# Output projection as seven products of half blocks, with layer 0's division on ScalarE and its rows read back from DRAM

## The chip, the cores and the metric

The kernel runs on one core of a Trainium2 chip. The metric is the device time of a whole execution in microseconds (us). TensorE (PE in the profile; PEld is its weight load) multiplies matrices into PSUM, VectorE (DVE) and ScalarE (ACT) do elementwise work, GpSimd (POOL) does small work here, and SyncE (SP) issues the DMAs.

## The reference

Two layers of attention over 64 graphs of 256 nodes with 512 features, all float32, eight heads of 64. Each layer adds its input and normalises:

```python
# layer 0: graph attention
feats = einsum('bnf,hfu->bhnu', X, W)
dense = leaky_relu(e_self[..., :, None] + e_neigh[..., None, :], 0.2) - 1e10 * (1 - A)
out0 = relu(einsum('bhij,bhju->bhiu', softmax(dense), feats) + b)
x = layernorm(x + out0)
# layer 1: attention mixed with adjacency and distance (both are adj here)
q, k, v = split(x @ W_qkv)
attn = softmax(q @ k.T * 64**-0.5) * 0.33 + 0.33 * adj + 0.33 * exp(-adj)
x = layernorm(x + (attn @ v) @ W_out + b_out)
```

(The node mask, all ones in the inputs, also enters layer 1.)

## The kernel before

The loop at the end of the kernel runs over the graphs b = 1 to 63 and calls two functions per round, between a `start` for the first two graphs and an `end`. One round works on four graphs at once: layer 0's attention of b, layer 0's projections of b + 1, layer 1's projections and scores of b - 1, and layer 1's values, output projection and normalisation of b - 2 and b - 3. Each call `do(stage, b, step)` emits one step of one stage, and `in_order` (L86) then ties each engine's instructions to the order of the source. So every engine's order is the order in which the `do` lines stand, and a step placed earlier or later moves on all engines that it uses.

The projections of both layers are done by `seven` (L289): a product of two matrices cut into half blocks, done in seven products of half blocks and additions, instead of eight products. `left_factors` (L273) forms four sums of the activation's half blocks on VectorE (`xC`, `hC`), and `right_factors` (L215) the same for weights, once. In `seven`, the products p1, p6, p7 and p4 add up one after the other in one PSUM bank ("chain"); ScalarE copies the bank (L309) after each of them, so that each copy must be done before the next of these products may write. p2 has a bank of its own, p5 and p3 share a third, and `add` (L312) adds these onto the copies on VectorE:

```python
BANK = dict(p1="chain", p6="chain", p7="chain", p4="chain", p2="alone", p5="pair", p3="pair")
COPIES = dict(p1=11, p6=12, p7=22, p4=21)
ADDED = {11: "alone", 22: "pair", 12: "pair"}
```

The output projection `project` (L1004) is a plain one: for each of the two blocks of 128 rows, four products of 128 x 128 with 128 x 512 into one bank. (A float32 product is two instructions in the profile.) `sum_up` (L932) adds the residual, which lies in `X1[b]`, straight from PSUM.

The other steps that this text names: `scores` (L811) computes the scores of two heads and ScalarE exponentiates them (L826); `pairs` (L834) adds two blocks of them; `values` (L916) multiplies weights and values, ScalarE copies the result to `oT` (L930). `rows` (L477) turns two columns of layer 0's features into rows and takes their maximum on VectorE; `broadcast` (L488) exponentiates them on ScalarE ("grow", L490) and sends them through DRAM to all partitions. `row_sums` (L857) and `invert` (L863) compute the inverse row sums of layer 1's softmax and send them through DRAM ("rb"). `columns` (L540) forms layer 0's column factors ("nd", then "ccol" on ScalarE), `scaled` (L607) scales the features on ScalarE, `weights` of layer 0 (L641) forms the attention weights `pT` on VectorE (L650), and `product` (L661) multiplies. `norm0` (L681) divides by the row sums: a reciprocal (L686) and a multiplication (L688), both on VectorE, into `X1[b]`. `end` (L694) adds the input, and `squares` and `norm` normalise on ScalarE with small steps on POOL. `weights` of layer 1 (L903) multiplies the probabilities by the inverse row sums and adds the common part. `rows_to_blocks` (L773) stores layer 0's rows to a DRAM buffer `hs` and reads them back in blocks `hb`, which VectorE transposes to `hT` (L121).

SBUF and PSUM buffers come from pools: a tile with a tag and `bufs=n` waits until one of its n buffers is released. [...] At the end of a round, `ps_tile([P, F], f"turn_{b}")` takes an "mm" buffer without using it.

## Time and profile before

| | us |
|---|---|
| median of 3 runs | 2964.55 (2962.11 to 2969.35) |
| profiled execution | 2961.33 |
| its span, first to last instruction | 2959.6 |
| TensorE busy | 2922.9 |
| VectorE busy | 2609.2 |
| ScalarE busy | 1468.1 |
| GpSimd busy | 185.6 |

The mean granted TensorE clock is 0.994. The DMA queues moved 328 MB. Busy times of different engines overlap; only the engine that is never idle, or a chain of waits between engines, sets the end. A line number such as L300 in a profile line is one of the kernel before; the changed kernel's numbers are some 8 to 90 higher.

### The profile page before, as it was taken

Reading aid. Unit: us, or ns where it says so; the run is one execution under the profiler, and the core shown is the slowest. Engines: PE = TensorE matmul, PEld = TensorE weight load, DVE = VectorE, ACT = ScalarE, POOL = GpSimd, SP = SyncE. Lnnn points to the kernel's source line nnn. Section 1 sums busy time; section 2 is a strip of 40 time slices with the busy share of each in tenths; the row PEclk is TensorE's granted clock in tenths of the full one; section 3 lists DMA queues with packets and bytes.
Section 4 is the critical chain, followed back from the end, with each engine's and each line's share of the span. In section 5 each row is a group of like instructions: output and inputs, shape, how many; then the busy total and the mean of one; then the engine's idle time right before and its main releaser. Section 6 shows DMA issues by size and latency. Waiting matters only on the chain.

```text
span 2959.6 us, 64542 instructions
## 1 busy us (share of the span) xinstructions
PE 2922.9 (99%) x25526; PEld 2321.6 (78%) x25526; DVE 2609.2 (88%) x5151; ACT 1468.1 (50%) x3585; POOL 185.6 (6%) x526
## 2 busy tenths in 40 slices
PE   8999999999999999999999999999999999999998
PEld 6787877877878878778778778778788787787785
DVE  5898898898998988989988988989889889889884
ACT  2445555555455455455555554554554554555443
POOL 0000000000000000000000000000000000000000
PEclk8999999999999999999999999999999999999999
DMA  6344454454444444444544543544444445445421
GB/s 137 79 121 109 106 130 104 103 137 95 112 128 102 114 116 105 124 109 106 130 107 105 132 101 106 134 98 112 122 104 118 111 107 126 109 105 131 102 87 50
DMA packets 760611, 328.20 MB, mean 111 GB/s; under 512 B 693516, under 2 KB 694268, under 8 KB 744312
## 3 DMA queue, kind: packets, MB, share of 16 engines
q1 hardware_dynamic: 758200, 323.55, 44.0%
q8 instruction: 204, 3.34, 0.5%
q14 instruction: 95, 0.78, 0.1%
q10 hardware_dynamic: 2112, 0.52, 0.1%
HBM read 256.13 MB, written 67.61 MB: 109 GB/s over the span
## 4 chain that ended last, share of the span: by engine, by line
PE 96%; DVE 1%; DMA 1%; issue 0%; ACT 0%; SPq 0%; POOL 0%; POOLq 0%; DVEq 0%
PE pq_p L300 27%; PE po L1007 15%; PE pv_p L300 13%; PE pf_p L300 13%; PE av L673 8%; PE pz L817 8%; PE av L922 8%; PE pd L846 2%; PE pr L82 1%; PE pg L531 0%; SPq L114 0%; DMA gb<-gs 0%; DMA rb<-rs 0%; DMA x<-in_x_dram 0%; DMA xb<-in_x_dram 0%
## 5 line engine op out<-in xcount | busy, mean ns | idle before, releaser
L300 PE MATMUL pq_p<-hC,wqk_sb 128*128 128x128 f32 x4096 | 489.1, 278 | 6.0 <-ACT qk L309 3.9
L300 PEld LDWEIGHTS pq_p<-hC,wqk_sb 128*128 128x128 f32 x4096 | 470.6, 193 | 11.8 <-ACT qk L309 4.7
L1007 PE MATMUL po<-wo_sb,oT 128*128 128x512 f32 x1024 | 450.0, 592 | 0.0
L650 DVE SCALAR_TENSOR_TENSOR pT<-gb,ccol,at 128x256 f32<-128x256 f32 x992 | 403.2, 478 | 17.5 <-ACT ccol L549 17.5
L351 ACT ACTIVATE junk<-x,nmean_l 128x512 bf16<-128x512 f32 x256 | 185.0, 722 | 418.5 <-POOL nmean_l L346 414.4
L300 PEld LDWEIGHTS pq_p<-hT,wqk_sb 128*128 128x128 f32 x3072 | 355.0, 193 | 28.7 <-issue 25.5
L300 PE MATMUL pq_p<-hT,wqk_sb 128*128 128x128 f32 x3072 | 372.7, 278 | 2.1 <-DVE hT L121 0.7
L826 ACT ACTIVATE p<-pz,hide 128x512 f32<-128x512 f32 x512 | 309.8, 688 | 123.8 <-PE av L922 106.1
L1007 PEld LDWEIGHTS po<-wo_sb,oT 128*128 128x128 f32 x1024 | 189.7, 190 | 216.5 <-issue 200.2
L912 DVE TENSOR_TENSOR p<-p,ct 128x1024 f32<-128x1024 f32 x252 | 308.7, 1225 | 8.6
L309 ACT COPY qk<-pq_p 128x512 f32<-128x512 f32 x256 | 147.2, 575 | 328.2 <-PE pq_p L300 328.2
L905 DVE TENSOR_TENSOR p<-p,rb 128x1024 f32<-128x1024 f32 x252 | 304.2, 1207 | 5.3 <-DMA rb<-rs 5.3
L309 ACT COPY v<-pv_p 128x256 f32<-128x256 f32 x256 | 95.3, 372 | 336.2 <-PE pv_p L300 336.2
L673 PE MATMUL av<-v,pT 128*64 128x65 f32 x8192 | 256.6, 223 | 3.7 <-issue 2.9
L817 PE MATMUL pz<-qk 64*128 64x256 f32 x2048 | 256.3, 389 | 2.2 <-ACT p L826 2.1
L673 PEld LDWEIGHTS av<-v,pT 128*64 128x64 f32 x8192 | 246.8, 139 | 13.0 <-issue 5.3
L609 ACT ACTIVATE v<-v 128x64 f32<-128x64 f32 x1024 | 251.6, 337 | 0.0
L300 PE MATMUL pf_p<-wf_sb,xC 128*128 128x264 f32 x992 | 251.1, 386 | 0.0
L300 PE MATMUL pv_p<-wv_sb,hC 128*128 128x256 f32 x1024 | 242.3, 379 | 0.0
L817 PEld LDWEIGHTS pz<-qk 64*128 64x128 f32 x2048 | 187.1, 186 | 66.7 <-ACT p L826 27.3
L922 PE MATMUL av<-p,v 128*64 128x256 f32 x2016 | 231.7, 382 | 0.0
L300 PEld LDWEIGHTS pv_p<-wv_sb,hC 128*128 128x128 f32 x1024 | 194.4, 190 | 27.9 <-ACT v L309 0.4
(137 smaller groups left out, 3775.0 us busy)
## 6 DMA issues: line engine op xcount, KB each, us to landing
rb<-rs SPq DMA_DIRECT2D x63, 1024.0 KB, 5.4
gb<-gs SPq DMA_DIRECT2D x62, 1028.0 KB
xb<-in_x_dram SPq DMA_DIRECT2D x252, 128.0 KB, 5.6
x<-in_x_dram SPq DMA_DIRECT2D x63, 512.0 KB
hs<-x SPq DMA_DIRECT2D x63, 512.0 KB
hb<-hs SPq DMA_DIRECT2D x252, 128.0 KB, 3.4
out_dram<-x SPq DMA_DIRECT2D x63, 512.0 KB, 5.5
adj<-in_adj_dram SPq DMA_DIRECT2D x256, 64.0 KB, 4.4
```

What stands on the lines that cost most here:

```text
L300: matmul(d, lhsT, rhs, start=(p in FIRST and i == 0), stop=(i == len(todo) - 1), skip_group_check=True,)
L309: nc.scalar.copy(out[COPIES[p]], dst)
L351: nc.scalar.activation(junk, self.src[:, t, :], AF.Square, bias=self.nmean[:, t : t + 1], accum_out=self.rstd[:, t : t + 1],)
L609: nc.scalar.activation(V0[b][:, t, h, :U], V0[b][:, t, h, :U], AF.Copy, scale=V0[b][:, t, h, U : U + 1],)
L650: nc.vector.scalar_tensor_tensor(pT[h][:, j, :], GB[b][h], CCOL[b][:, j, h : h + 1], AT[b][:, j, :], op0=ALU.max, op1=ALU.mult,)
L673: matmul(av[r * half : (r + 1) * half, k, :], pT[h][:, j, i : i + half], V0[b][:, j, h, :UA], start=(j == 0), stop=(j == T - 1),)
L817: matmul(pz[:, r, j, :], QK[b][rows, g, 1, j * P : (j + 1) * P], QK[b][rows, g, 0, :], start=True, stop=True,)
L826: nc.scalar.activation(p[:, :, j, :], pz[:, :, j, :], AF.Exp, bias=hide[:, j, b : b + 1], scale=U**-0.5,)
L905: nc.vector.tensor_mul(p, p, REC[b][:, k : k + 2, g // 2, :] .unsqueeze(2) .to_broadcast([P, 2, T, N]),)
L912: nc.vector.tensor_add(p, p, CT[b].unsqueeze(1).to_broadcast([P, 2, T, N]))
L922: matmul(av[0][r * U : (r + 1) * U, g % 2, :], V1[b][:, j, 2 * g + r, :], PROBS[b][g][:, r, j, :], start=(j == 0), stop=(j == T - 1),)
L1007: matmul(po, oT[:, c, t * P : (t + 1) * P], wo_sb[:, c, :], start=(c == 0), stop=(c == C - 1),)
```

## The change

The output projection of graphs 0 to 61 goes through `seven_rows`: `half_blocks` forms the left factors of `oT` on VectorE, the products go to `o` (in the buffer of tag "xb", which the loads of the next input blocks use too), ScalarE copies and VectorE adds, and `sum_up` follows in the next round from SBUF. The last two graphs keep the plain form, with products 256 wide, since `wo_sb` now holds the seven right factors. Layer 0's rows, which were kept in `X1` with three buffers, are read back from `hs` into `Y[b]` for the residual, and `X1` has one buffer. The division of layer 0 is done on ScalarE from graph 2 on, as sixteen activations of 64 columns with the reciprocal as scale. The copy of the inverse row sums (`zd`) goes to ScalarE. In the order of the source, `bias`, `aT`, the left factors of x and of h, the loads of the next blocks and the store of layer 1 stand elsewhere, the squares of layer 0 are split in two, and the unused PSUM tile is gone.

```diff
@@ -158,3 +158,3 @@
     load_wf(nc.scalar, 0)
-    a_bc = io.tile([P, 2, H, U], FT, tag="x1", name="a_bc", bufs=3)
+    a_bc = io.tile([P, 2, H, U], FT, tag="x1", name="a_bc", bufs=1)
     for k, a in enumerate((a_self, a_neigh)):
@@ -181,3 +181,3 @@
     bo_bc = consts.tile([P, F], FT, name="bo_bc")
-    wo_sb = consts.tile([P, C, F], FT, name="wo_sb")
+    wo_sb = consts.tile([P, 7, C2, F2], FT, name="wo_sb")
 
@@ -232,2 +232,10 @@
 
+    def load_wo():
+
+        wo12 = work.tile([P, C2, F2], FT, tag="pT", name="wo12", bufs=4)
+        parts = w_out.rearrange("(k c p) (g f) -> k g p c f", k=2, p=P, g=2)
+        for dst, k, g in ((wo_sb[:, 0], 0, 0), (wo12, 0, 1), (wo_sb[:, 1], 1, 0), (wo_sb[:, 2], 1, 1)):
+            nc.sync.dma_start(dst, parts[k, g])
+        return wo12
+
     def load_weights1():
@@ -682,3 +690,3 @@
             if b not in X1:
-                X1[b] = io.tile([P, T, F], FT, tag="x1", name=f"x1_{b}", bufs=3)
+                X1[b] = io.tile([P, T, F], FT, tag="x1", name=f"x1_{b}", bufs=1)
             av = AV[g][:, t, : HG * UA].rearrange("p (h u) -> p h u", u=UA)
@@ -686,8 +694,18 @@
             nc.vector.reciprocal(rec, av[:, :, U])
-            s = slice(g * HG * U, (g + 1) * HG * U)
-            nc.vector.tensor_mul(
-                X1[b][:, t, s].rearrange("p (h u) -> p h u", u=U),
-                av[:, :, :U],
-                rec.unsqueeze(2).to_broadcast([P, HG, U]),
-            )
+            if b < 2:
+                s = slice(g * HG * U, (g + 1) * HG * U)
+                nc.vector.tensor_mul(
+                    X1[b][:, t, s].rearrange("p (h u) -> p h u", u=U),
+                    av[:, :, :U],
+                    rec.unsqueeze(2).to_broadcast([P, HG, U]),
+                )
+                return
+            for k in range(HG):
+                h = g * HG + k
+                nc.scalar.activation(
+                    X1[b][:, t, h * U : (h + 1) * U],
+                    av[:, k, :U],
+                    AF.Copy,
+                    scale=rec[:, k : k + 1],
+                )
 
...
@@ -730,3 +748,3 @@
             hb = io.tile([P, C, N // B, B], FT, tag="hb", name=f"hb_{b}", bufs=1)
-            hs = dram.tile([N, F], FT, tag="hs", name=f"hs_{b}")
+        HS[b] = dram.tile([N, F], FT, tag="hs", name=f"hs_{b}", bufs=4)
 
@@ -773,4 +791,5 @@
         def rows_to_blocks():
-            nc.sync.dma_start(hs.rearrange("(t p) f -> p t f", p=P), X1[b])
-            load_blocks(hb, hs)
+            nc.sync.dma_start(HS[b].rearrange("(t p) f -> p t f", p=P), X1[b])
+            if b > 0:
+                load_blocks(hb, HS[b])
 
@@ -778,3 +797,2 @@
             transpose_blocks(hT, hb)
-            left_factors(hC, hT)
 
@@ -876,3 +894,7 @@
             )
-            nc.vector.tensor_copy(zd, inv.unsqueeze(2).to_broadcast([P, K, B]))
+            nc.scalar.copy(zd, inv.unsqueeze(2).to_broadcast([P, K, B]))
+            PD["blocks"] = zd
+
+        def inverted():
+            zd = PD["blocks"]
             rec = work.tile([P, 2, N], FT, tag="rec1", name=f"rec1_{b}", bufs=1)
...
@@ -931,10 +955,16 @@
 
+        def rows_again():
+
+            tag = "y" if b < NB - 2 else "hb"
+            Y[b] = io.tile([P, T, F], FT, tag=tag, name=f"y_{b}", bufs=1)
+            nc.sync.dma_start(Y[b], HS[b].rearrange("(t p) f -> p t f", p=P))
+
         def sum_up(po, t):
             if t == 0:
-                NORM["l1", b] = LayerNorm(X1[b], b, "l1")
+                NORM["l1", b] = LayerNorm(Y[b], b, "l1")
             nc.vector.scalar_tensor_tensor(
-                X1[b][:, t, :],
+                Y[b][:, t, :],
                 po,
                 1.0,
-                X1[b][:, t, :],
+                Y[b][:, t, :],
                 op0=ALU.mult,
@@ -948,2 +978,21 @@
 
+        SEVEN = {}
+
+        def half_blocks():
+            oC = work.tile([P, 4, C2, P], FT, tag="xC", name=f"oC_{b}", bufs=1)
+            left_factors(oC, oT)
+            SEVEN["o"] = o = io.tile([P, T, F], FT, tag="xb", name=f"o_{b}", bufs=1)
+            SEVEN["product"], SEVEN["add"] = seven_rows(
+                f"po_{b}",
+                oT,
+                oC,
+                wo_sb,
+                [P, F2],
+                {
+                    10 * (t + 1) + g + 1: o[:, t, g * F2 : (g + 1) * F2]
+                    for t in range(T)
+                    for g in range(2)
+                },
+            )
+
         LAST = {}
@@ -999,4 +1048,6 @@
         def residual():
+            if b == NB - 1:
+                Y[b] = X1[b]
             nc.vector.tensor_add(
-                X1[b], X1[b], bo_bc.unsqueeze(1).to_broadcast([P, T, F])
+                Y[b], Y[b], bo_bc.unsqueeze(1).to_broadcast([P, T, F])
             )
@@ -1004,11 +1055,14 @@
         def project(t):
+
             po = ps_tile([P, F], f"po_{b}_{t}")
-            for c in range(C):
-                matmul(
-                    po,
-                    oT[:, c, t * P : (t + 1) * P],
-                    wo_sb[:, c, :],
-                    start=(c == 0),
-                    stop=(c == C - 1),
-                )
+            wo = [[wo_sb[:, 0], WO["12"]], [wo_sb[:, 1], wo_sb[:, 2]]]
+            for g in range(2):
+                for c in range(C):
+                    matmul(
+                        po[:, g * F2 : (g + 1) * F2],
+                        oT[:, c, t * P : (t + 1) * P],
+                        wo[c // C2][g][:, c % C2],
+                        start=(c == 0),
+                        stop=(c == C - 1),
+                    )
             sum_up(po, t)
...
@@ -1032,2 +1086,7 @@
             project=project,
+            rows_again=rows_again,
+            half_blocks=half_blocks,
+            product=lambda p: SEVEN["product"](p),
+            product_add=lambda i: SEVEN["add"](i),
+            sum_up=lambda t: sum_up(SEVEN["o"][:, t, :], t),
             squares=lambda *ts: NORM["l1", b].squares(*ts),
@@ -1117,2 +1176,3 @@
         do("proj1", 0, "from_rows", 1)
+        do("proj1", 0, "blocks")
         do("proj1", 0, "hC")
@@ -1145,3 +1205,3 @@
         if b > 1:
-            do("attend1", b - 3, "squares")
+            do("attend1", b - 4, "squares")
             do("proj1", b - 1, "qk", "p1")
@@ -1149,3 +1209,4 @@
             do("proj0", b, "columns")
-            do("attend1", b - 3, "store")
+            do("attend1", b - 4, "store")
+            do("attend1", b - 3, "rows_again")
             do("proj1", b - 1, "qk", "p6")
@@ -1162,2 +1223,4 @@
             do("proj1", b - 1, "qk_add", 22)
+            if b + 1 < NB:
+                do("turned", b + 1, "xC")
             do("attend1", b - 2, "weights", 0)
@@ -1170,15 +1233,16 @@
             nc.sync.dma_start(bo_bc, b_out.partition_broadcast(P))
-            nc.sync.dma_start(wo_sb, w_out.rearrange("(c p) f -> p c f", p=P))
+            WO["12"] = load_wo()
             in_order()
-        for g in range(2):
-            for t in range(T):
-                do("attend0", b, "norm0", g, t)
-        do("attend0", b, "end")
-        if b + 2 < NB:
-            load(b + 2)
+        for t in range(T):
+            do("attend0", b, "norm0", 0, t)
         if b > 1:
             do("proj1", b - 1, "qk", "p4")
+        for t in range(T):
+            do("attend0", b, "norm0", 1, t)
+        if b > 1:
             do("proj1", b - 1, "qk", "p3")
-            do("proj1", b - 1, "qk_add", 12)
         do("attend1", b - 2, "weights", 1)
+        if b > 1:
+            do("proj1", b - 1, "qk_add", 12)
+        do("attend0", b, "end")
         do("proj1", b - 1, "values", "p1")
@@ -1186,2 +1250,3 @@
         do("proj1", b - 1, "v_add", 11)
+        do("attend1", b - 3, "residual")
         do("proj1", b - 1, "values", "p6")
@@ -1190,9 +1255,15 @@
         do("proj1", b - 1, "v_add", 22)
+        for t in range(T):
+            do("attend1", b - 3, "sum_up", t)
+        if b + 2 < NB:
+            load(b + 2)
         do("proj0", b + 1, "product", "p1")
         do("proj1", b - 1, "values", "p4")
+        do("attend1", b - 2, "weights", 2)
+        do("attend0", b, "squares", slice(0, 1))
         do("proj0", b + 1, "product", "p6")
+        do("attend0", b, "squares", slice(1, 2))
         do("proj1", b - 1, "values", "p3")
-        do("attend0", b, "squares")
-        do("attend1", b - 2, "weights", 2)
         do("proj1", b - 1, "v_add", 12)
+        do("proj0", b + 1, "aT")
         do("proj0", b + 1, "product", "p5")
@@ -1205,4 +1276,2 @@
         do("proj0", b + 1, "product", "p2")
-        do("proj0", b + 1, "add", 11)
-        do("proj0", b + 1, "aT")
         if b + 2 < NB:
@@ -1213,2 +1282,3 @@
         do("attend1", b - 2, "weights", 3)
+        do("proj0", b + 1, "add", 11)
         do("proj0", b + 1, "add", 12)
@@ -1223,3 +1293,2 @@
         do("softmax1", b - 1, "both", 1)
-        do("proj0", b + 1, "bias")
         if b + 2 < NB:
@@ -1228,2 +1297,3 @@
             do("attend1", b - 2, "values", g)
+        do("attend1", b - 2, "half_blocks")
         do("softmax1", b - 1, "scores", 2)
@@ -1234,11 +1304,21 @@
         do("proj0", b + 1, "broadcast")
-        do("attend1", b - 2, "residual")
-        do("attend1", b - 2, "project", 0)
+        do("attend1", b - 2, "product", "p1")
+        do("attend1", b - 2, "product", "p2")
         do("proj1", b, "hT")
-        do("attend1", b - 2, "project", 1)
+        do("attend1", b - 2, "product_add", 11)
+        do("attend1", b - 2, "product", "p6")
+        do("attend1", b - 2, "product", "p5")
+        do("attend1", b - 2, "product", "p7")
+        do("attend1", b - 2, "product_add", 22)
+        do("proj1", b, "hC")
         do("softmax1", b - 1, "sums")
         do("softmax1", b - 1, "invert")
-        if b + 2 < NB:
-            do("turned", b + 2, "xC")
-        ps_tile([P, F], f"turn_{b}")
+        do("attend1", b - 2, "product", "p4")
+        do("proj0", b + 1, "bias")
+        do("softmax1", b - 1, "inverted")
+        do("attend1", b - 2, "product", "p3")
+        do("attend1", b - 2, "product_add", 12)
+        if b == 1:
+            right_factors(wo_sb, WO.pop("12"))
+            in_order()
 
@@ -1248,4 +1328,10 @@
         do("proj1", b, "qk", "p1")
-        do("attend1", b - 2, "squares")
-        do("attend1", b - 2, "store")
+        do("attend1", b - 3, "squares")
+        do("attend1", b - 3, "store")
+        do("attend1", b - 2, "rows_again")
+        do("attend1", b - 1, "rows_again")
+        WO["12"] = work.tile([P, C2, F2], FT, tag="pT", name="wo12_again", bufs=4)
+        nc.sync.dma_start(
+            WO["12"], w_out.rearrange("(k c p) (g f) -> k g p c f", k=2, p=P, g=2)[0, 1]
+        )
         do("proj1", b, "qk", "p2")
@@ -1265,4 +1351,5 @@
         do("attend1", b - 1, "values", 1)
-        do("attend1", b - 1, "residual")
-        do("attend1", b, "residual")
+        do("attend1", b - 2, "residual")
+        do("attend1", b - 2, "sum_up", 0)
+        do("attend1", b - 2, "sum_up", 1)
         do("softmax1", b, "scores", 0)
...
```

## The prediction

> **What bounds it now.** I read the page first: engine shares, chain, costliest groups.
>
> ```profile
> span 2959.6 us, 64542 instructions
> PE 2922.9 (99%) x25526; PEld 2321.6 (78%) x25526; DVE 2609.2 (88%) x5151; ACT 1468.1 (50%) x3585; POOL 185.6 (6%) x526
> ...
> PE 96%; DVE 1%; DMA 1%; issue 0%; ACT 0%; SPq 0%; POOL 0%; POOLq 0%; DVEq 0%
> ...
> L1007 PE MATMUL po<-wo_sb,oT 128*128 128x512 f32 x1024 | 450.0, 592 | 0.0
> ...
> L609 ACT ACTIVATE v<-v 128x64 f32<-128x64 f32 x1024 | 251.6, 337 | 0.0
> ```
>
> TensorE is the bound: 99% busy and 96% of the chain. The projection (L1007) is 450 us of it. VectorE, at 88%, has little to give. Then I cut out one steady period with the windows view (us; then busy of PE, PEld, DVE, ACT, POOL, with instruction counts; granted clock; DMA share; GB/s):
>
> ```profile
> 1483.19:1528.11 44.92, 44.92 (x398) 35.73 (x397) 40.66 (x81) 22.89 (x56) 2.82 (x8) 1.00 0.45 113
> ```
>
> A period is 44.92 us, TensorE never idles, VectorE has 4.3 us free. Last, the timeline of it (start, duration, engine, line), where the order is read:
>
> ```profile
> 1496.75 0.69 DVE L838 SCALAR_TENSOR_TENSOR both<-p 128x512 f32<-128x512 f32 x1 [0.30 <-ACT p L826]
> ...
> 1499.14 7.03 PE L1007 MATMUL po<-wo_sb,oT 128*128 128x512 f32 x16
> ...
> 1500.32 0.47 ACT L490 ACTIVATE grow<-pr,nb 8x256 f32<-8x256 f32 x1
> ...
> 1506.10 1.07 PE L846 MATMUL pd<-both,ones 128*32 128x256 f32 x16
> ...
> 1507.30 0.72 ACT L351 ACTIVATE junk<-x,nmean_l 128x512 bf16<-128x512 f32 x1 [6.52 <-POOL nmean_l L346]
> ...
> 1511.49 3.26 DVE L650 SCALAR_TENSOR_TENSOR pT<-gb,ccol,at 128x256 f32<-128x256 f32 x8 [0.28 <-ACT ccol L549]
> ...
> 1513.35 3.93 ACT L609 ACTIVATE v<-v 128x64 f32<-128x64 f32 x16
> ...
> 1521.42 0.18 DVE L686 RECIPROCAL rec<-av 128x4 f32<-128x4 f32 x1
> ...
> 1522.20 0.58 ACT L309 COPY qk<-pq_p 128x512 f32<-128x512 f32 x1 [4.46 <-PE pq_p L300]
> ...
> 1523.79 1.89 PE L300 MATMUL pv_p<-wv_sb,hT 128*128 128x256 f32 x8
> ...
> 1524.85 0.37 ACT L309 COPY v<-pv_p 128x256 f32<-128x256 f32 x1 [2.07 <-PE pv_p L300]
> ...
> 1525.52 2.75 PE L300 MATMUL pv_p<-wv_sb,hC 128*128 128x256 f32 x12
> ```
>
> Three things to see. ScalarE's copies follow TensorE closely: p1 of the values ends about 1524.65, its copy runs 1524.85 to 1525.22, and p6, which adds onto the same bank, starts at 1525.52, with 0.3 us to spare. ScalarE's idle time (6.52 and 4.46 us) lies just before such copies. And the reciprocals at 1521.42 come late in VectorE's order.
>
> [...] The trace shows each engine in source order. [...] The trace's L609 agrees: 337 ns, sixteen in 3.93 us, one each 246. [...] I keep clock 1.00; no stretch of this period tests it.
>
> **The parts, per period.** My clock is 0 at the first scores product (trace 1491.24); "free" is when TensorE would be ready.
>
> *Projection.* Sixteen 512-wide instructions, with their lead-in, hold TensorE from 1499.03 to the row sums at 1506.10: 7.07 us. Seven products of two half blocks are 28 instructions of 256; the twelve of the values run from 1525.52 to the next product at 1528.11, 0.216 each. 28 x 0.216 = 6.05: **-1.02 us**. Batches 0 to 61 get it; the last two use 32 of 256, 6.9 us, even.
>
> *VectorE.* Added: four left factors of oT (1.48, by hC's steps), three adds of halves (0.40 each). Gone: four multiplications (0.38 each in step) and the zd copy (0.46). The two sum-ups stay. Net 1.48 + 1.20 - 1.52 - 0.46 = **+0.7 us**, 41.4 of 43.9: it fits as a sum. What counts is the order.
>
> *ScalarE.* Added: four copies of 256 (0.37 each), sixteen divisions (16 x 0.246 = 3.93), the zd copy (0.58 by L309 of that size[...]). 22.9 + 6.0 = 29 of 44: free as a sum, not in place.
>
> *Wait 1, p6 of the projection.* It needs the copy of p1, queued behind the grow exponential, which waits for VectorE's maximum. VectorE: pair sums end 6.1, xT 1.17, the new left factors 1.48, maximum to exponential 0.63 (1499.69 to 1500.32): 9.4; exponential 0.47, copy 0.37: 10.3. TensorE is free at 9.5. **+0.8.**
>
> *Wait 2, p6 of the queries.* Projection p6, p5, p7 end 12.9; copy 13.5; add 22 13.9; hC 1.48, zd, reciprocal and mask 1.26: 16.65. ScalarE then does the zd copy 0.58, the copy of p4 0.37, layer 1's squares 1.66 (before, they were done by 1509.0) and only then the queries' p1, 0.58: 19.9. Free at 19.3. **+0.65.** Behind it ccol, 0.22: VectorE starts the weights L650 at 20.2.
>
> *Wait 3, p6 of the values.* VectorE: weights and two adds 7.7 (3.26 + 0.6 + 3.25 + 0.6), left factors of x now here 1.45, weights 0 2.42, reciprocal 0.2: 31.95. ScalarE, stopped on that reciprocal, then does eight divisions 1.97, the copy of p4 0.57, eight divisions 1.97, the copy of the values' p1 0.37: 36.9. Free at 33.3 + 0.8 + 0.65 = 34.7. **+2.25.** The rest of the period is 10.6 of TensorE: 47.6.
>
> *Moved steps and queues.* SP: the xb loads (four) now wait for the sum-up that frees their buffer, at about 42; their 2.6 us of issue end before the hs store at 47, and xT needs them 11 us later: nothing, by that slack. Read-back: one 512 KB issue, behind the out store's landing (median 5.5), about 28 to 33, wanted at 38: nothing; it holds SP, where only the xb loads are behind it. POOL: squares in two parts, three more small operations, about 1.1 us; the norm still precedes the hs store. Bias, hT, aT and the store one batch later are reorderings, inside the VectorE sums or on queues with slack. One x1 buffer: the hs store has read it long before the next divisions. The dropped PSUM placeholder and four issues for w_out: nothing. Right factors of w_out: four of 0.7 once, up to +3 us, left out. What the trace can't price is the step of a division out of PSUM and each hand-over; ends 0.20 to 0.28 a division and 0.3 us over the three waits: 0.7 either way. I take L609's 0.246.
>
> **Sum.** -1.02 + 0.8 + 0.65 + 2.25 = +2.7 us, times 62 periods = +167. The profiled execution took 2961.3 us (span 2959.6 and 1.7 around it), 3.2 below the median of the runs; the difference carries over: 2964.5 + 167 = **3132 us**.
>
> **The rivals.** About 0.3% (9 us, 0.14 a period) is the least that a measurement of this kernel tells from no change.
>
> *Work alone (0.15).* Waits 1 and 2 and VectorE's own waits vanish. Its work alone puts the reciprocal at about 29.9, the values' copy at 35.0 against free 33.3: 1.7 - 1.02 = +0.7, 3008; with cheap divisions 0. For it: VectorE has slack; against: each wait hangs on a FIFO order. The range of this case is 2965 to 3040.
>
> *The gain arrives (0.06).* ScalarE's values copy comes in time, and the period is TensorE's 43.9: 62 x 1.02 = 63 less, 2901. It decides at one place: the first reciprocal must stand by about 28.1 on my clock (33.0 less 4.9 of divisions and copy). For: TensorE is the bound and ScalarE half idle; against: before, it stood at 30.2, and VectorE's work ahead of it is nearly the same.
>
> *DMA too late (0.06).* The xb loads land after 53 (or read-back after 38), TensorE waits for VectorE some 1.3 us more: 3132 + 80 = 3212. Against: 11 us of slack, and DMA is idle before hs.
>
> The change not doing what it says: only if the products were not 28, which the source excludes.
>
> **Numbers.** Likeliest (0.73): 3132, with 0.7 a period either way 3088 to 3176. Range 3030 to 3185: the upper end of work alone, all of the likeliest, some of the DMA case. Faster 0.06; same 0.03 (low end of work alone); slower 0.91.
>
> **What would show it.** Right: TensorE idle before p6 of the values by about 2.2 us a period, waiting for a ScalarE copy whose queue waited for the reciprocal; two waits under 1 us at p6 of projection and queries; po at about 6.05 us of work; TensorE's share near 92%; VectorE's busy time up some 45 us. Wrong: a period under 44.9; divisions far from 0.25 us; the longest TensorE waits on DMA, or at a place not named here.

## The result, and the profile after

The changed kernel takes **3178.1 us** (median of 4 runs, 3171.1 to 3182.6) against 2965.3 for the kernel before in the same session: ratio **1.0715**, 95% interval 1.0687 to 1.0743. The forecast was 3132, range 3030 to 3185. The profiled execution took 3182.5 us. Its busy times and its chain of waits read:

```profile
PE 2958.1 (93%) x26302; PEld 2485.4 (78%) x26302; DVE 2611.4 (82%) x5277; ACT 1772.6 (56%) x4889; POOL 423.6 (13%) x715
...
DVE 35%; ACT 17%; PE 16%; DMA 14%; POOL 9%; issue 5%; SPq 4%; DVEq 0%; ACTq 0%; POOLq 0%
```

TensorE fell from 96% of the chain to 16%. It is still busy for 93% of the span, so the first line alone would suggest that little has changed; the chain shows that it now follows the others. POOL went from 185.6 to 423.6 us of busy time, with 715 instructions instead of 526.

The timeline of one period, at the places that the prediction named (its clock 0 is 1601.46 here):

```profile
1611.28 0.34 ACT L317 COPY o<-po_p 128x256 f32<-128x256 f32 x1
...
1611.67 2.86 PE L308 MATMUL po_p<-wo_sb,oC 128*128 128x256 f32 x12 [0.42 <-ACT o L317]
...
1632.90 0.18 DVE L694 RECIPROCAL rec<-av 128x4 f32<-128x4 f32 x1
1633.12 0.93 ACT L705 ACTIVATE x<-av,rec 128x64 f32<-128x64 f32 x4 [4.71 <-DVE rec L694]
...
1634.07 0.25 DVE L694 RECIPROCAL rec<-av 128x4 f32<-128x4 f32 x2 [0.99 <-ACT x L705]
1634.17 1.89 PE L308 MATMUL pv_p<-wv_sb,hT 128*128 128x256 f32 x8
...
1636.56 0.18 DVE L694 RECIPROCAL rec<-av 128x4 f32<-128x4 f32 x1 [2.23 <-ACT x L705]
...
1636.77 0.93 ACT L705 ACTIVATE x<-av,rec 128x64 f32<-128x64 f32 x4 [0.25 <-DVE rec L694]
1637.57 0.39 ACT L317 COPY v<-pv_p 128x256 f32<-128x256 f32 x1
...
1638.01 2.86 PE L308 MATMUL pv_p<-wv_sb,hC 128*128 128x256 f32 x12 [1.95 <-ACT v L317]
...
1643.87 1.22 DVE L929 TENSOR_TENSOR p<-p,rb 128x1024 f32<-128x1024 f32 x1
...
1644.04 1.12 POOL L354 TENSOR_SCALAR nmean_l<-sums_l 128x2 f32<-128x2 f32 x1 [2.80 <-DVE y L965]
```

What to see: TensorE waits before the sixth product of the projection and, longer, before that of the values, each time for a ScalarE copy (the brackets give the idle time and its releaser). ScalarE itself stood idle for 4.71 us until the first reciprocal. It keeps to the order of the source: the values' first product had ended at 1636.06, but ScalarE stood idle for 0.25 us until the last reciprocal, divided, and only then, at 1637.57, copied. New is the other direction: the second and the fourth reciprocal wait 0.99 and 2.23 us for ScalarE's divisions. New, too, is the last line: a GpSimd operation on 128 x 2 numbers takes 1.12 us beside a VectorE multiplication of two SBUF tiles and ends 0.07 us after it.

The waits of the whole run (engine and line, what it waited for: total us, times, longest):

```profile
ACT x L705 <- DVE rec L694: 339.9, 186, 6.8
...
DVE rec L694 <- ACT x L705: 199.9, 124, 2.2
...
PE pv_p L308 <- ACT v L317: 134.7, 65, 2.6
...
DVE nd L550 <- DMA gb<-gs: 60.2, 50, 2.6
PE po_p L308 <- ACT o L317: 55.4, 60, 1.4
DVE ct L459 <- ACT far L450: 43.6, 42, 1.0
```

The prediction had rows one, three and five; rows two, four and six it had not. (`far` is the exponential of the adjacency, and `ct` the common part of layer 1's weights that VectorE forms from it.) Measured from row sums to row sums, the 60 steady periods last 48.58 us on average, from 47.3 to 50.6; before, they were 44.92 nearly always, 45.03 on average. So the period is about 1.3 us longer than the shortest one, and the shortest one alone is near the timetable of the prediction (47.6). The windows view of two periods (us, then busy time of PE, PEld, DVE, ACT and POOL with counts, granted clock, DMA share, GB/s):

```profile
1601.46:1648.76 47.30, 44.90 (x409) 37.83 (x408) 40.09 (x82) 27.40 (x77) 5.84 (x10) 1.00 0.46 119
1502.81:1552.47 49.66, 46.58 (x409) 39.09 (x409) 41.32 (x83) 28.21 (x78) 7.72 (x13) 0.97 0.45 113
```

The long one has a granted clock of 0.97. Cut into windows of 2 us around its wait for the values (sixth product at 1540.04), it shows where:

```profile
1538.81:1540.81 2.00, 0.77 (x4) 0.69 (x5) 1.97 (x2) 1.18 (x5) 0.00 (x0) 1.00 0.00 0
1540.81:1542.81 2.00, 2.00 (x8) 1.62 (x7) 2.00 (x5) 0.37 (x1) 0.00 (x0) 0.65 0.00 0
1542.81:1544.81 2.00, 2.00 (x6) 1.63 (x5) 1.74 (x5) 0.37 (x1) 0.22 (x1) 0.50 0.00 0
```

TensorE works through the last two, at half clock.

### The profile page after: what moved, and what is told of

Same layout as the page of the kernel before. It is cut to its first block, busy times and chain, and to the rows that moved or that the text cites. A ratio compares the mean times of both kernels' runs of the same rounds, so it can differ in the third digit from the quotient of the medians.

```text
span 3180.7 us, 68341 instructions
## 1 busy us (share of the span) xinstructions
PE 2958.1 (93%) x26302; PEld 2485.4 (78%) x26302; DVE 2611.4 (82%) x5277; ACT 1772.6 (56%) x4889; POOL 423.6 (13%) x715
## 4 chain that ended last, share of the span: by engine, by line
DVE 35%; ACT 17%; PE 16%; DMA 14%; POOL 9%; issue 5%; SPq 4%; DVEq 0%; ACTq 0%; POOLq 0%
DVE pT L658 8%; DMA gb<-gs 7%; ACT x L705 6%; PE pv_p L308 4%; DVE p L929 4%; PE pf_p L308 3%; POOL rstd_l L370 3%; DMA gs<-grow 3%; SPq L114 3%; DVE qk L320 3%; PE po_p L308 3%; DVE p L936 3%; ACT v L617 3%; POOL rstd_l L367 2%; DVE y L965 2%
## 5 line engine op out<-in xcount | busy, mean ns | idle before, releaser
L658 DVE SCALAR_TENSOR_TENSOR pT<-gb,ccol,at 128x256 f32<-128x256 f32 x992 | 403.3, 479 | 26.1 <-ACT ccol L557 26.1
L705 ACT ACTIVATE x<-av,rec 128x64 f32<-128x64 f32 x992 | 232.2, 325 | 339.9 <-DVE rec L694 339.9
L308 PE MATMUL pv_p<-wv_sb,hC 128*128 128x256 f32 x1024 | 277.2, 419 | 134.0 <-ACT v L317 133.7
L308 PEld LDWEIGHTS pq_p<-hT,wqk_sb 128*128 128x128 f32 x3072 | 361.5, 193 | 6.0 <-DVE hT L121 1.7
L308 PEld LDWEIGHTS pv_p<-wv_sb,hC 128*128 128x128 f32 x1024 | 206.9, 207 | 191.5 <-ACT v L317 159.0
L844 ACT ACTIVATE p<-pz,hide 128x512 f32<-128x512 f32 x512 | 311.8, 704 | 28.1 <-PE av L946 21.9
L936 DVE TENSOR_TENSOR p<-p,ct 128x1024 f32<-128x1024 f32 x252 | 308.7, 1225 | 8.6
L929 DVE TENSOR_TENSOR p<-p,rb 128x1024 f32<-128x1024 f32 x252 | 305.1, 1211 | 4.3 <-DMA rb<-rs 4.3
L308 PE MATMUL po_p<-wo_sb,oC 128*128 128x256 f32 x992 | 240.7, 385 | 55.4 <-ACT o L317 55.4
L354 POOL TENSOR_SCALAR nmean_l<-sums_l 128x2 f32<-128x2 f32 (+1 forms) x130 | 84.1, 647 | 1546.2 <-DVE x L717 1284.3
L308 PEld LDWEIGHTS po_p<-wo_sb,oC 128*128 128x128 f32 x992 | 183.4, 190 | 102.3 <-ACT o L317 79.8
L367 POOL TENSOR_SCALAR rstd_l<-rstd_l 128x1 f32<-128x1 f32 (+1 forms) x193 | 98.4, 510 | 1175.3 <-ACT junk L359 1165.2
L617 ACT ACTIVATE v<-v 128x64 f32<-128x64 f32 x1024 | 251.6, 337 | 0.0
```

Source lines behind the costliest of these rows:

```text
L308: matmul(d, lhsT, rhs, start=(p in FIRST and i == 0), stop=(i == len(todo) - 1), skip_group_check=True,)
L367: nc.gpsimd.tensor_scalar(rstd, rstd, 1.0 / F, EPS, op0=ALU.mult, op1=ALU.add)
L617: nc.scalar.activation(V0[b][:, t, h, :U], V0[b][:, t, h, :U], AF.Copy, scale=V0[b][:, t, h, U : U + 1],)
L658: nc.vector.scalar_tensor_tensor(pT[h][:, j, :], GB[b][h], CCOL[b][:, j, h : h + 1], AT[b][:, j, :], op0=ALU.max, op1=ALU.mult,)
L705: nc.scalar.activation(X1[b][:, t, h * U : (h + 1) * U], av[:, k, :U], AF.Copy, scale=rec[:, k : k + 1],)
L844: nc.scalar.activation(p[:, :, j, :], pz[:, :, j, :], AF.Exp, bias=hide[:, j, b : b + 1], scale=U**-0.5,)
```

## The experiments

All ratios are to the kernel before on the same chip. "Period" is the commonest length from row sums to row sums (mean in brackets where it differs by more than 0.1).

| kernel | us, median | ratio, 95% interval | period, us |
| --- | --- | --- | --- |
| before | 2965 to 2968 | 1 | 44.92 (45.03) |
| changed | 3178.1 | 1.0715, 1.0687 to 1.0743 | 48.0 (48.58) |
| changed, e1: reciprocals early | 2969.9 | 1.0007, 0.9998 to 1.0015 | 45.08 |
| changed, e2: division on VectorE | 3071.4 | 1.035, 1.0327 to 1.0373 | 46.5 (46.81) |
| changed, e3: squares whole | 3135.9 | 1.0559, 1.054 to 1.0578 | 47.32 (47.77) |
| changed, e4: copy first | 3167.4 | 1.0666, 1.0644 to 1.0688 | uneven (48.41) |
| e1 with e4: e5 | 2933.8 | 0.9888, 0.9874 to 0.9901 | 44.39 (44.56) |
| e6: all orders | **2921.8** | **0.9843, 0.9829 to 0.9856** | 44.24 |
| before, e7: ScalarE divides, in place | 3027.6 | 1.0202, 1.0188 to 1.0216 | 46.08 |
| changed, e8: wait filled | 3173.3 | 1.069, 1.0675 to 1.0704 | 48.0 (48.38) |
| e6, e9: rows read back twice | 2923.7 | 0.985, 0.9836 to 0.9863 | 44.24 |
| before, e10: ScalarE divides, early | 2966.0 | 0.9996, 0.9987 to 1.0004 | 44.92 (45.07) |
| e3 with e8: e11 | 3111.4 | 1.0486, 1.0468 to 1.0503 | 47.32 |
| changed, e12: reciprocals joined, late | 3067.4 | 1.0338, 1.0323 to 1.0354 | 46.63 |

### The reciprocals early (e1)

My theory: the first reciprocal stands too late in VectorE's order. The rival: the added work itself is too much. The edit takes one reciprocal per half of the heads, for both row blocks, and puts both right after the attention products that they read in the source: the first ahead of the left factors of x, the second behind these and ahead of the first of layer 1's weights. The divisions stay.

```diff
-            if b + 1 < NB:
-                do("turned", b + 1, "xC")
-            do("attend1", b - 2, "weights", 0)
         for g in range(2):
             for t in range(T):
                 do("attend0", b, "product", g, t)
+        if b > 1:
+            do("attend0", b, "inverse0", 0)
+            if b + 1 < NB:
+                do("turned", b + 1, "xC")
+            do("attend0", b, "inverse0", 1)
+            do("attend1", b - 2, "weights", 0)
...
-            do("attend0", b, "norm0", 0, t)
+            do("attend0", b, "norm0" if b < 2 else "divided0", 0, t)
```

> The changed kernel with the same work, but the reciprocals of layer 0 (one per half of the heads instead of two) stand on VectorE before the left factors of x and before weights 0, so about 4 us earlier in the period. Order theory (the copy of the values' p1 is late because the divisions wait for a reciprocal behind other VectorE work): the wait before p6 of the values, 2.1 us in a period of the changed kernel, goes to under 0.3; with it the half-speed stretches of TensorE after it; 62 periods times 2.1 to 3.0 us less than 3178: 2990 to 3050. Work theory (ScalarE and VectorE simply have too much to do): nothing changes, 3165 to 3190.

Measured: 2969.9 us, 208 less. Its timeline:

```profile
1522.65 0.20 DVE L719 RECIPROCAL rec<-av 128x8 f32<-128x8 f32 x1
...
1528.85 0.37 ACT L317 COPY v<-pv_p 128x256 f32<-128x256 f32 x1 [0.42 <-PE pv_p L308]
...
1529.51 2.75 PE L308 MATMUL pv_p<-wv_sb,hC 128*128 128x256 f32 x12
```

The copy now waits for TensorE (0.42), not TensorE for the copy: the twelve instructions carry no bracket. The period is 45.08 nearly throughout. The same work, in another order, is no slower than the kernel before: the theory of too much work falls. The edit does two things at once, though: it places the reciprocals early, and it makes two of four. The last experiment (e12) takes the joining alone.

### The division back on VectorE (e2)

```diff
-            if b < 2:
+            if b < NB:
                 s = slice(g * HG * U, (g + 1) * HG * U)
```

> The changed kernel with layer 0's division back on VectorE (one multiplication of 256 columns per half) in the place where the reciprocals stand; all else as changed. Order theory: ScalarE reaches the copy of the values' p1 without waiting for a reciprocal, the wait before p6 of the values goes, VectorE gets 1.5 us more work a period but loses its own 3.2 us of waits between reciprocals: 2980 to 3050. If VectorE's load were the cause, the 1.5 us come on top: 3178 + 62 x 1.5 = 3270. If the seven products or the read-back were the cause, nothing is gained: 3178.

Measured: 3071.4, halfway. The wait for the values' copy is gone, but the gain falls short of what was expected: VectorE leads the chain with 39% (DMA has 19%, TensorE 12%), it waits 74.5 us for gb and 62.5 for `far`, and the projection's sixth product still waits 67. Taking the suspected step out leaves a second limit, of which TensorE is a small part.

### The squares of layer 0 in one piece (e3)

GpSimd's small operations take 647 ns each in the mean for the negative means (L354; the same line, L346 before, 218). In the changed kernel's trace they are long where they run beside a VectorE instruction with two SBUF tiles: L354 above starts 0.17 us after the multiplication L929, which takes two, and ends 0.07 us after it. So do all 61 of the 130 operations of L354 that take over 0.7 us (1.12 to 1.13 each). Another 63 start inside an addition with one operand in PSUM (L320), and take 0.22 to 0.23. What makes them long the trace does not show. My theory was that this time reaches the period. The edit puts the squares back in the order of the kernel before, whole, with the third of layer 1's weights behind them.

```diff
-        do("attend1", b - 2, "weights", 2)
-        do("attend0", b, "squares", slice(0, 1))
         do("proj0", b + 1, "product", "p6")
-        do("attend0", b, "squares", slice(1, 2))
         do("proj1", b - 1, "values", "p3")
+        do("attend0", b, "squares")
+        do("attend1", b - 2, "weights", 2)
```

> The changed kernel with the squares of layer 0 in one piece and weights 2 behind them, as they stood before the change. [...] (GpSimd's small operations are stretched where they run beside VectorE's operations with two inputs in SBUF; 424 us busy against 186 before, and the normalisation, the adjacency exponentials and the scores' exponentials follow late): GpSimd's busy time falls to 250 to 320 us, 0.4 to 0.9 us a period are won: 3120 to 3155. If GpSimd's time is hidden: 3170 to 3190 with the busy time down all the same.

Measured: 3135.9, 42 us less, as this theory asked; POOL's busy time fell from 423.6 to 269.1 us, and VectorE no longer waits for `far` in forming the common part `ct`. The lines of GpSimd in the changed kernel and, second, in e3:

```profile
L354 POOL TENSOR_SCALAR nmean_l<-sums_l 128x2 f32<-128x2 f32 (+1 forms) x130 | 84.1, 647 | 1546.2 <-DVE x L717 1284.3 <-DVE y L965 220.3 <-DVE rec L694 41.1
...
L354 POOL TENSOR_SCALAR nmean_l<-sums_l 128x2 f32<-128x2 f32 (+1 forms) x130 | 84.3, 649 | 1528.4 <-DVE x L717 1267.1 <-DVE y L965 221.4 <-DVE rec L694 39.4
```

L354 is as slow in e3 as in the changed kernel, so the 42 us did not come from it. What became shorter are the three operations behind the squares (L367 from 510 to 428 ns in the mean, L370 from 808 to 699, L371 from 438 to 290), and there are 189 fewer of them. The edit also moves the squares on ScalarE and a part of the weights on VectorE. So the 42 us are the price of the split squares as a whole; how much of it is GpSimd beside VectorE, and how much the number or the order of the operations, is not parted.

### The copy ahead of the exponential (e4), and both (e5)

```diff
-        do("proj0", b + 1, "broadcast")
         do("attend1", b - 2, "product", "p1")
+        do("proj0", b + 1, "broadcast")
```

> The changed kernel with p1 of the projection, and with it ScalarE's copy of it, ahead of the exponential of the row factors (grow) in the source. Order theory: the wait before p6 of the projection (about 0.6 us, 55 us of TensorE in all and more at its weight load) goes to under 0.15, and since the reciprocals hang behind this product through the later copies, all of it arrives: 62 x 0.4 to 0.9 us, 3120 to 3155. If this wait is only moved to the next one: 3170 to 3185.

Measured: 3167.4, just under the second expectation. The wait at the projection's sixth product is gone, but only 11 us came of it: VectorE, with its column terms, now waits 102.2 us for gb instead of 60.2. The wait moved on. It is not that the exponential which sends gb on its way became late: counted from the first scores product it starts at 10.1 us in both kernels (median of 30 periods). With the early reciprocals it was another matter:

> Both orders in one kernel: the reciprocals of layer 0 ahead of the left factors of x and the weights (2969.9 us alone), and the copy of the projection's first product ahead of the broadcast and its exponential (3167.4 alone, 11 us less than the changed kernel). If the two waits stand one after the other in the chain and the later wait for the column sums was only a guest of the stalled period, the 0.42 us that the projection's sixth product still waits come out of each of 62 periods of 45.08 us: 2940 to 2950 us. If the copy's move is answered by a later exponential and a later normalized row, as it was alone, it gives what it gave there or nothing: 2960 to 2970 us.

Measured: 2933.8, 36 us below e1, slightly more than the higher of the two expectations. The period fell from 45.08 to 44.39: 0.69 us, where the bracket in the trace showed 0.42 (a product's end is modelled, so the idle time shown may be too low). The same edit is worth 11 us or 36, depending on which loop sets the period.

### All orders together (e6)

e1, e3 and e4 in one kernel; besides, the rows' maximum is taken ahead of the left factors of the projection, so that the exponential isn't late, and layer 1's squares move from the start of the next round to the place ahead of `hC`. Cut to what e1, e3 and e4 don't have:

```diff
-            do("attend1", b - 4, "squares")
...
-        do("attend1", b - 2, "half_blocks")
         do("softmax1", b - 1, "scores", 2)
         do("softmax1", b - 1, "scores", 3)
         do("proj0", b + 1, "rows")
+        do("attend1", b - 2, "half_blocks")
+        do("attend1", b - 2, "product", "p1")
+        do("proj0", b + 1, "broadcast")
         do("softmax1", b - 1, "both", 2)
         do("softmax1", b - 1, "both", 3)
-        do("proj0", b + 1, "broadcast")
-        do("attend1", b - 2, "product", "p1")
...
+        do("attend1", b - 3, "squares")
         do("proj1", b, "hC")
...
-        do("attend1", b - 3, "squares")
         do("attend1", b - 3, "store")
```

> All three orders: reciprocals early, the copy of the projection's first product ahead of the broadcast with the rows' maximum taken before the products so that the column terms aren't sent later, and the squares of layer 0 in one piece with those of layer 1 in the idle time of ScalarE ahead of the queries. If waits of TensorE were all that kept the seven half products from paying, the period falls by the 1.02 us of the two products less what it has already got: from 45.08 us to about 44.2 to 44.5, so 2905 to 2940 us, below the kernel before. If TensorE's other work sets the period (it is busy for 98% of it already in the kernel with early reciprocals), it stays at 2955 to 2970 us.

Measured: 2921.8, 1.6% below the kernel before: the best version found. A period in the windows view, then the projection in the timeline of TensorE:

```profile
1481.88:1526.12 44.24, 44.24 (x410) 37.93 (x409) 40.66 (x81) 28.09 (x77) 3.67 (x8) 1.00 0.54 128
```

```profile
1521.56 1.89 PE L308 MATMUL po_p<-wo_sb,oT 128*128 128x256 f32 x8
1523.36 2.83 PE L308 MATMUL po_p<-wo_sb,oC 128*128 128x256 f32 x12
1526.12 1.07 PE L886 MATMUL pd<-both,ones 128*32 128x256 f32 x16
1527.12 1.13 PE L308 MATMUL po_p<-wo_sb,oT 128*128 128x256 f32 x4
1528.09 1.03 PE L308 MATMUL po_p<-wo_sb,oC 128*128 128x256 f32 x4
1528.95 3.73 PE L308 MATMUL pq_p<-hT,wqk_sb 128*128 128x128 f32 x32
```

The profile shows TensorE busy for all of the period: no wait is left that another order could take away. The 28 instructions take 4.56 us up to the row sums and 1.83 after them, 6.39 or 0.228 each, not the 0.216 of the prediction. The period is 0.68 below that of before, not 1.02.

### Eight products, division on ScalarE (e7 and e10)

The kernel before with the division on ScalarE, in its old place (e7) and with the early, joined reciprocals (e10, the same steps as e1):

```diff
-            nc.vector.tensor_mul(
-                X1[b][:, t, s].rearrange("p (h u) -> p h u", u=U),
-                av[:, :, :U],
-                rec.unsqueeze(2).to_broadcast([P, HG, U]),
-            )
+            for k in range(HG):
+                h = g * HG + k
+                nc.scalar.activation(
+                    X1[b][:, t, h * U : (h + 1) * U],
+                    av[:, k, :U],
+                    AF.Copy,
+                    scale=rec[:, k : k + 1],
+                )
```

> The kernel before with one edit: layer 0's division of the later rounds on ScalarE in the place where VectorE had it; eight products, no read back. By the order theory the reciprocals stand behind the left factors of x and the divisions behind the reciprocals, the copy of the values' first product comes late, and each period gets some 1.75 to 2.5 us more: 3065 to 3120 us. By the theory that the seven products or the rows read back from DRAM make the changed kernel slow, this edit alone costs nothing: 2960 to 2975 us.

> The kernel before (eight products, no read back) with layer 0's division on ScalarE and the reciprocals early, one per half for both row blocks. It tells what the seven products are worth: with eight, TensorE has 44.92 us of work a period, and if no wait is left the time is that of the kernel before, 2960 to 2970 us, some 43 us above the kernel with all three orders. If instead the orders themselves made that one fast, this one comes below 2950 us too. If ScalarE's divisions still come late ahead of the values, above 2975 us.

Measured: e7 3027.6, e10 2966.0. In e7's timeline the wait is that of the changed kernel, shorter:

```profile
1416.34 0.18 DVE L686 RECIPROCAL rec<-av 128x4 f32<-128x4 f32 x1
...
1421.50 2.86 PE L300 MATMUL pv_p<-wv_sb,hC 128*128 128x256 f32 x12 [0.89 <-ACT v L309]
```

So the division on ScalarE costs 60 us by itself, without seven products or read back, though less than the order theory asked: 1.16 us a period (46.08 less 44.92), not 1.75. That expectation had a slip: in the kernel before, the left factors of x do not stand ahead of the reciprocals. The first one starts at 30.2 us from the first scores product in e7, as in the kernel before, and at 31.4 in the changed kernel. e10 takes the cost back whole. And e10 against e6, eight products against seven (with the read back) where no order hinders either, is what the change could give: 44 us.

### The read back doubled (e9)

```diff
-            nc.sync.dma_start(Y[b], HS[b].rearrange("(t p) f -> p t f", p=P))
+            for _ in range(2):
+                nc.sync.dma_start(Y[b], HS[b].rearrange("(t p) f -> p t f", p=P))
```

> The kernel with all three orders (2921.8 us), the rows of layer 0 read back from DRAM twice into the same tile instead of once: one more 512 KB transfer and one more issue on SP in each period. If the read back is hidden, as the prediction took it, nothing changes: 2915 to 2930 us. If its traffic, or SP held for it, delays the loads or the broadcast that the column terms wait for, a second one must cost something: above 2935 us.

Measured: 2923.7, with intervals that overlap e6's. A second transfer of 512 KB per period is hidden there, so the first is. In the changed kernel, where a loop through the DMAs is the longer one, this was not run; but VectorE stands idle for 0.0 us in all ahead of its 63 first uses of the rows read back (L1051).

### The wait filled with work (e8 and e11)

The long period above suggested that the half clock makes the changed kernel slow. The second product of the values is computed three times into its own bank, which fills 1.73 us of the wait (eight times 0.216, an estimate; the wait falls from about 2.1 us to 0.5 in the mean).

```diff
-        do("proj1", b - 1, "values", "p2")
+        do("proj1", b - 1, "values", "p2", 3)
...
-            for i, (d, lhsT, rhs) in enumerate(todo):
+            for i, (d, lhsT, rhs) in times * list(enumerate(todo)):
```

> The changed kernel with the second product of the values computed three times over into its own bank, so that TensorE works through most of the wait ahead of the sixth: eight more instructions of 0.216 us, 1.73 us a period, 107 us in all. The output is unchanged. By the clock theory (after some 2 us of idle TensorE runs at half speed for a few us, in about a third of the periods) the wait is filled, the granted clock comes back from 0.98 to above 0.99, and the time falls by some 20 periods of 1.5 to 2 us: 3135 to 3155 us, faster with more work. If the waits alone set the time and the clock costs nothing, the filling is hidden and it stays at 3171 to 3185. If the filling isn't hidden, it adds up to 107: 3200 to 3285.

Measured: 3173.3, 5 us below the changed kernel, with intervals that overlap. The mean granted clock came back from 0.984 to 0.995, and it changed nothing: my theory of the clock, as the cause in this kernel, fell. The chain of this run shows the reason:

```profile
DVE 41%; DMA 19%; ACT 14%; POOL 11%; issue 6%; PE 5%; SPq 5%; DVEq 0%; ACTq 0%; POOLq 0%
DVE pT L658 11%; DMA gb<-gs 9%; ACT x L705 5%; DVE p L929 4%; DMA gs<-grow 4%; POOL rstd_l L370 4%; SPq L114 4%; DVE qk L320 3%; DVE p L936 3%; DMA hb<-hs 3%; POOL rstd_l L367 3%; DVE y L965 2%; DVE x L717 2%; DVE y L1051 2%; POOL nmean_l L354 2%
```

TensorE is 5% of it. The chain goes round through the column terms, the weights L658, the divisions, VectorE's sums for layer 0's rows, GpSimd's layer norm, the hs store and load, and the way of grow through DRAM to the next column terms; that loop takes about 48.0 us. Half clock in TensorE is hidden by the slack that TensorE has there. The test had to be made where TensorE leads, so e11 has the fill and e3's squares:

> The fill of the values' wait (two more copies of the second product, 1.73 us a period) on top of the squares in one piece. With the squares whole (3135.9 us alone) a period is 47.32 us mostly and 49.0 in about a quarter of them, a mean of 47.77, and TensorE leads the chain. If those longer periods are the half clock after an idle TensorE, and the fill alone changed nothing only because another loop, through GpSimd and the DMAs, set the period there, the long periods go: 62 times 0.45, 28 us less, 3105 to 3115 us. If the half clock costs nothing in itself, 3130 to 3140. If the fill isn't hidden, above 3150.

Measured: 3111.4, 24.5 us below e3, with the clock up from 0.985 to 0.993. In e3 the periods are 47.32 us and, in 15 of 60, about 49.0, and these 15 are those with a clock below 1.00; with the fill they are gone. There the half clock was worth 24.5 us, and a kernel that computes more was faster.

### The reciprocals joined but late (e12)

```diff
+        if b > 1:
+            do("attend0", b, "inverse0", 0)
+            do("attend0", b, "inverse0", 1)
         for t in range(T):
-            do("attend0", b, "norm0", 0, t)
+            do("attend0", b, "norm0" if b < 2 else "divided0", 0, t)
```

> The changed kernel with one reciprocal for both row blocks of a half, both halves at once, in the late place where the first reciprocal stands (after the left factors of x and the weights); four reciprocals become two, and VectorE no longer stops between them. It parts the late start of the divisions, which stays, from the 3.2 us in each period that VectorE waits inside them. By my sum the late start is all: the values' copy comes only some 0.5 us sooner (two hand-overs less), 47.3 to 46.8 us a period, and with the clock 3120 to 3150 us. If VectorE's 3.2 us, which lie ahead of its sums for layer 0's rows and so of the layer norm and the hs store, set the outer loop of 48.0 us, the outer loop falls below TensorE's and the clock decides: the same 3120 to 3150 with the mean wait for gb down from 60 us to under 30. If the early place is not needed at all, 2970 to 3000, as with early reciprocals.

Measured: 3067.4, half of e1's gain, and more than I expected. In its timeline the two reciprocals stand together, still late, and TensorE's wait is 1.28:

```profile
1528.32 0.27 DVE L719 RECIPROCAL rec<-av 128x8 f32<-128x8 f32 x2
...
1532.20 0.50 ACT L317 COPY v<-pv_p 128x256 f32<-128x256 f32 x1
...
1532.75 2.86 PE L308 MATMUL pv_p<-wv_sb,hC 128*128 128x256 f32 x12 [1.28 <-ACT v L317]
```

The wait for gb fell from 60.2 to 24.9, so the outer loop no longer leads, and the clock is 0.993: with waits of mostly 1.28 us the long periods are gone too. Of e1's 208 us, 111 came from joining the reciprocals and 97 from their place, if the steps are taken in this order; four separate reciprocals in the early place were not run.

## Why the prediction was right, and which terms were off

The sign, the place and the mechanism were right: TensorE waits before the sixth products for ScalarE copies that stand in a queue behind the division, which waits for a late reciprocal. That place decides: with the reciprocals at 27.6 (e1) instead of 31.4 on the prediction's clock, the loss is gone, as the rival "the gain arrives" said of 28.1. (Its 2901 us did not come, since wait 1 stays in e1 and the products save less.)

That the total fell inside the range is in part luck. It is 46 us above the forecast and 2 above the band of the likeliest case (3088 to 3176). What lifted it are two terms that the prediction had at nothing; the room above the band had been kept for late DMAs.

The table goes by periods, from the kernel before to e6, e5, e1, e3 and the changed kernel. Not every step is one edit: e5 and e6 differ in several orders, and e1 has the squares in parts, which e3 has not.

| term of the sum, us a period | predicted | measured |
| --- | --- | --- |
| projection | -1.02 | -0.68 (44.92 to 44.24) |
| rest of orders, wait 2 among it | +0.65 | +0.15 (44.24 to 44.39) |
| wait 1, projection p6 | +0.8 | +0.69 (44.39 to 45.08) |
| wait 3, values p6 | +2.25 | +2.24 (45.08 to 47.32) |
| half clock, where TensorE leads | 0 | +0.45 (47.32 to 47.77) |
| squares in parts, outer loop | 0 | +0.81 (47.77 to 48.58) |

The measured terms add up to 3.66 us a period, 227 in 62 periods, against 213 measured. Of the difference, 7 us are that the kernel before has a mean of 45.03 and not 44.92; the rest was not traced.

- **Projection**: the steady step of the values' twelve instructions was taken for all 28. In e6's four groups, of 8, 12, 4 and 4, they took 0.228 each in the mean. The change's own worth is 0.68 a period, some 42 us (44 by e10 against e6), of which the changed kernel kept nothing.
- **Wait 1** was right within about 0.1 (its own terms add up to 10.2, not 10.3). **Wait 2** hardly came: in the period above the queries' copy ends at 19.5, not 19.9, and p6's weight load waits 0.22.
- **Wait 3** came out right as a size: from the end of the reciprocal to the end of the copy 4.95 us were predicted, and 1633.08 to 1637.96 is 4.9. (By its own terms the wait adds up to 2.1, not 2.25.) But this is two errors that cancel. The divisions out of PSUM follow each other at about 0.20 us (eight of them take 1.75 in e12, four 0.93), not at 0.246, which takes some 0.7 off the sixteen. And the four reciprocals and the divisions wait for each other: without that, in e12, the same way is 4.1 us (1528.59 to 1532.70) and the period 0.69 shorter. The prediction called both unpriced and allowed 0.20 to 0.28 a division, which holds, and 0.3 for the hand-overs of all three waits, which is too little.
- **ScalarE's idle time**: of the two stretches named, the 6.52 us lay ahead of layer 1's squares, which waited for GpSimd, and not of a copy. No term rests on it.
- **"I keep clock 1.00"** failed. It was an assumption that no stretch of the period looked at had tested; waits near 2 us brought half clock (0.50) in some periods (18 of 60 in the changed kernel).
- **"POOL: three more small operations, about 1.1 us; the norm still precedes the hs store"** failed: POOL's work per period went from 2.82 us to 5.84 in the short period, and the layer norm came late enough for the loop through hs and gb to pass TensorE's. The cost was counted as instructions times their old duration, but beside VectorE's instructions with two SBUF tiles the duration changed (L354 from 218 ns to 647 in the mean).
- **VectorE "up some 45 us"**: it rose by 2 (2609.2 to 2611.4). The left factors (102 us over four rows) and additions (73) were priced rightly, at 175 us against 166, but more went away: 105 of multiplications, 27 of the zd copy and some 10 of reciprocals and sum-ups, 142. By the groups of instructions VectorE has 28 us more, but its records overlap more, so that the busy time shows 2. The forecast doesn't rest on it. TensorE's share of 93% against 92% agrees in the number alone: its busy time rose from 2922.9 to 2958.1 us instead of falling, in part because the same 409 instructions count 46.58 us in a period with half clock and 44.90 in one without.
- The **read back** at nothing was right (e9). The rival of work alone lost to e1; that of late DMAs was near in one respect: the outer loop does pass through DMA, but what made it late stands ahead of it: on GpSimd and VectorE (e3), and in the divisions that the layer norm waits for (e12).

The table depends on the order in which the kernels are compared; e12 takes out the outer loop and the clock together with 0.69 of wait 3, so the last two rows aren't independent of it. Why the second reciprocal of a half waits for divisions that read other rows of the same PSUM tile stays open: the trace shows the wait, and not whether the chip needs it or only the program's semaphores ask for it.

## What to carry to other kernels

When work moves to an engine with idle time, ask what it waits for and what stands behind it in that engine's queue; then move the releasing instruction first. Here joining four small reciprocals into two was worth 111 us, and moving these ahead of other work on VectorE another 97, each more than the whole saving in products. After removing a wait, read the chain again: as long as a second loop of nearly the same length leads, a right edit shows little (e4 gave 11 us, then 36; filling the wait gave 5, then 24.5).

## What the hardware showed that was not expected

- TensorE's clock fell to 0.50 after waits of about 2 us in 15 of 60 periods of e3, and in none of 60 in e12, with waits of mostly 1.28 us. In e3 the length of the wait doesn't decide: two waits of 2.58 us brought no half clock, one of 1.92 did, and of those of 1.97 some did and most did not. All changes of the clock in the changed kernel's trace stand on one grid of 3.413 us, and so do, within 0.04 us, those of e3 from 62 to 3000 us, which were read from windows of 2 us; in the steady periods each stretch at half clock lasts one step of it; half of that, 1.7 us, is what the long periods are longer (49.0 less 47.32). What decides which of these waits lower the clock was not shown.
- In the changed kernel 61 GpSimd operations of L354 that started inside VectorE's multiplication of two SBUF tiles (L929) took 1.12 to 1.13 us and ended 0.07 after it; 62 of L367 that started inside its addition of two SBUF tiles (L936) took 1.14 to 1.18 and ended 0.05 after it. Elsewhere the same lines took 0.22 to 0.23 and 0.19 to 0.25.
- ScalarE's divisions of 64 columns out of PSUM followed each other at about 0.20 us, the scalings of 64 columns in SBUF (L617) at 0.24.
- In this program two readers of one PSUM tile, VectorE's reciprocals and ScalarE's divisions of other rows, took turns: 199.9 us of VectorE waiting in 124 places, gone when the reciprocals were joined. The reason is open, as said above.
